# A cross-attention block on one core: steps over two pairs, seven products in more places, and the division moved from the weights to the context

## The chip, the cores and the metric

The kernel runs on one core of a Trainium2 chip. Its engines work side by side: TensorE (PE, with its weight loads as PEld), VectorE (DVE), ScalarE (ACT), GpSimd (POOL), and SyncE (SP), whose queue issues nearly all transfers. The metric is the device time of one launch in microseconds, lower is better; times are medians of runs.

## The reference

128 sequences of 128 tokens with 256 features attend to 128 sequences of context, with 16 heads of 16 features, and pass a feed-forward block with 1024 hidden features. All is float32.

```python
q = (query @ Wq + bq)    # heads: 16 x 16
k = (key @ Wk + bk)
v = (values @ Wv + bv)
scores = einsum('bhqd,bhkd->bhqk', q, k) / sqrt(16)
scores = where(j < i, scores, -1e30)          # mask == 0: strictly below the diagonal
attn = softmax(scores); attn[:, :, 0, :] = 0
ctx = einsum('bhqk,bhkd->bhqd', attn, v)
x = layer_norm(query + ctx @ Wo + bo, ln1_g, ln1_b)
ffn = relu(x @ W1 + b1) @ W2 + b2
out = layer_norm(x + ffn, ln2_g, ln2_b)
```

## The kernel before

Two sequences make a pair of 256 token columns; there are 64 pairs. Nothing loops on the chip: the program is written out in full, and the order in which each engine gets its instructions is the order in which Python emits them. The middle, pairs 7 to 62, is made of steps. One step (`steps`, from slot 9 to 60) runs the table `order` once: about 130 short names, each with a lag that says how many pairs back it works. The work on one pair is thus spread over several steps: scores and exponentials in its own step, the weighing of values at the end of the next, output and first norm two steps behind, H (W1) three behind, S (W2) four behind, the second norm five behind, and the store after that. The start and the end are written out call by call.

The names, with what they do for one pair:

- `q261`, `q457`, `q3`: the queries (class `Query`). The 256x256 matrix is cut into four 128x128 blocks and the 256 columns into two halves, and the product of the two by two blocks is made of seven block products instead of eight (1 to 7), with sums of blocks of Wq (once, `wqs`) and sums of the token blocks (`qs02`, `qs1`, `qs3`, on POOL, tile qS). DVE puts the seven together (`qC1`, `qU3`, `qC2`, `qC12`).
- `k`, `v`, `out`: keys, values and the output, four products of 256 columns each (`project`, `values`, `attention_out`). ACT copies the keys to kT four times (`copy_keys`, two halves of heads with zeros in between), the values to vz and vd.
- `H1` to `H7` (class `Hidden`): W1 by seven products; the two halves are the two sequences of the pair, so a matmul has 128 columns, and there are 4 x 7 of them. POOL makes the sums xS (`xs0` to `xs3`), ACT and DVE put the products together in hT, ACT adds the bias and takes the relu (`relu0` to `relu7`).
- `S1` to `S7` (class `Second`): W2 by seven products of four matmuls each, with sums hS on POOL (`hs0` to `hs3`). Six no-ops per pair are strewn between them on PE (`empty`).
- `scores`: 64 matmuls in strips of 32 rows, in all eight PSUM banks; `low`, `mask`, `max`, `lowmax` on DVE; `exp` and `lexp` on ACT with the row sums; `rcp` on DVE, and `sum0` to `sum2` on POOL, which multiply the weights (tile sm) by the reciprocals of their sums; `turn0` to `turn2`, transposes on DVE; `br0` to `br12`, sixteen transfers across partitions to pT; then `weigh` (tile pc) and `ctx`, ACT's copy of it to cxT.
- `tbx`, `x1out`, `x1in`: the normed tokens are transposed on DVE, written to DRAM by four transfers (x1t) and read back (x1T) for H.

The line that `Hidden` spends its matmuls on, and the one that POOL divides the weights by:

```python
ps[:, i * P : (i + 1) * P].rearrange("p (n a) -> p n a", a=32),
left(i), right, start=(i == 0 and which not in self.ONTO),
...
rs[:, :, None].to_broadcast([P, part.stop - part.start, n]), ALU.mult,
```

## Time and profile before

| | |
|---|---|
| median of 3 runs | 1477.11 us (1476.67 to 2419.54) |
| span of the profiled execution | 1476.5 us |
| granted TensorE clock in it | 0.999 |
| transfers | 206.22 MB, 140 GB/s in the mean |
| step of one pair in the middle | 22.45 us |

The profiled execution is the one whose spans and rows are quoted below. In the 40 slices of its span PE shows nine tenths or more in all but the last, POOL and DVE eight or nine in the middle, and ACT nine:

```profile
PE   9999999999999999999999999999999999999998
PEld 7788999999999999999999999999999999999998
DVE  7999899999998998998998999989989999999866
ACT  5758999999999999999999999999999999999863
POOL 7788999999999999999999999999999999999987
```

Rows of the chain give the start, the duration, the engine, the tile written, the line and the count of instructions. Rows of groups give line, engine, operation, tiles, shapes and count, then busy us and mean ns of one, then the idle time ahead of them and what ended it.

### The profile page before, as it was taken

What the parts mean: (1) busy time and instruction counts of PE and PEld (TensorE: products, weight loads), DVE (VectorE), ACT (ScalarE), POOL (GpSimd) and SP (SyncE); (2) the same over time, 40 slices, a digit from 0 to 9 for tenths busy, and PEclk for the clock granted to TensorE, in tenths of its full rate; (3) what the DMA queues carried; (4) which work ended last, traced back from release to release, by engine and by line L of the source; (5) the groups of instructions that cost most, each with busy time, mean ns of one, the idle gap of its engine ahead of it and who ended that gap; (6) DMA issues with size and microseconds to landing.
All of it is one profiled execution on the core that took longest, in us unless ns stands there. A gap on an engine that the chain in (4) does not pass through costs nothing.

```text
span 1476.5 us, 53972 instructions
## 1 busy us (share of the span) xinstructions
PE 1463.9 (99%) x19696; PEld 1377.8 (93%) x19696; DVE 1315.5 (89%) x2897; ACT 1323.0 (90%) x5279; POOL 1388.2 (94%) x1484
## 2 busy tenths in 40 slices
PE   9999999999999999999999999999999999999998
PEld 7788999999999999999999999999999999999998
DVE  7999899999998998998998999989989999999866
ACT  5758999999999999999999999999999999999863
POOL 7788999999999999999999999999999999999987
PEclk9999999999999999999999999999999999999999
DMA  8465566655656666666556566556565666664451
GB/s 203 96 141 127 133 146 139 147 138 136 156 141 138 141 146 139 148 144 145 138 135 154 139 142 141 144 135 157 141 139 136 146 141 150 136 152 122 116 162 58
DMA packets 417865, 206.22 MB, mean 140 GB/s; under 512 B 282434, under 2 KB 386114, under 8 KB 417602
## 3 DMA queue, kind: packets, MB, share of 16 engines
q1 hardware_dynamic: 416080, 202.49, 58.3%
q8 instruction: 159, 2.61, 0.8%
q14 instruction: 106, 0.85, 0.2%
q10 hardware_dynamic: 1520, 0.27, 0.1%
HBM read 71.84 MB, written 34.87 MB: 72 GB/s over the span
## 4 chain that ended last, share of the span: by engine, by line
PE 95%; DVE 1%; POOL 1%; DMA 1%; SPq 1%; issue 1%; ACT 0%; DVEq 0%; POOLq 0%
PE phs L1156 25%; PE pX L1064 11%; PE po L671 7%; PE pk L281 7%; PE pz L1064 7%; PE py L1064 7%; PE pv L411 7%; PE pq L351 6%; PE pss L502 6%; PE pc L652 4%; PE pc L642 3%; PE ph L917 1%; PE pq L281 1%; PE py L940 1%; SPq L608 1%; POOL sm L557 1%
## 5 line engine op out<-in xcount | busy, mean ns | idle before, releaser
L557 POOL TENSOR_TENSOR sm<-sm,rs 128x1024 f32<-128x1024 f32 x192 | 364.0, 1898 | 2.4 <-DVE rs L566 2.3
L997 ACT ACTIVATE sm<-pss,nmx 128x128 f32<-128x128 f32 x944 | 331.9, 395 | 8.4 <-DVE nmx L980 2.4
L997 ACT ACTIVATE sm<-sm,nmx 128x64 f32<-128x64 f32 x944 | 321.4, 361 | 0.8 <-DVE nmx L987 0.2
L1190 ACT ACTIVATE hT<-hT,b1e_c 128x256 f32<-128x256 f32 x480 | 216.1, 501 | 53.9 <-DVE hT L1181 44.7
L574 DVE STREAM_TRANSPOSE tb<-sm 128x1024 f32<-128x1024 f32 x186 | 227.8, 1226 | 1.5 <-POOL sm L557 1.4
L997 ACT ACTIVATION_READ_ACCUMULATOR sm<-pss,nmx 128x1 f32 x912 | 214.7, 235 | 0.0
L997 ACT ACTIVATION_READ_ACCUMULATOR sm<-sm,nmx 128x1 f32 x912 | 193.8, 212 | 0.0
L1156 PE MATMUL phs<-xS,w1t 128*128 128x128 f32 x1440 | 180.2, 275 | 0.0
L1156 PEld LDWEIGHTS phs<-xS,w1t 128*128 128x128 f32 x1440 | 170.4, 192 | 0.0
L980 DVE TENSOR_REDUCE nmx<-pss 128x4 f32<-128x512 f32 x236 | 160.6, 682 | 1.9
L401 ACT ACTIVATE kT<-pk,bkh,half 128x256 f32<-128x256 f32 x252 | 140.0, 559 | 4.1 <-PE pk L281 4.1
L516 DVE TENSOR_TENSOR sm<-pss,neg 128x256 f32<-128x256 f32 (+1 forms) x276 | 113.8, 436 | 16.5 <-PE pss L502 12.5
L1064 PE MATMUL pX<-wt,hS 128*128 128x128 f32 x960 | 126.8, 275 | 0.0
L1156 PE MATMUL phs<-x1T,w 128*128 128x128 f32 x960 | 126.5, 275 | 0.0
L1156 PEld LDWEIGHTS phs<-x1T,w 128*128 128x128 f32 x960 | 120.7, 192 | 3.0
L671 PE MATMUL po<-wo,cxT 128*128 128x256 f32 x512 | 121.8, 381 | 0.0
L411 PE MATMUL pv<-wv,cT 128*128 128x256 f32 x512 | 120.9, 379 | 0.0
L281 PE MATMUL pk<-cT,wk 128*128 128x256 f32 x504 | 119.5, 380 | 0.0
L1064 PEld LDWEIGHTS pX<-wt,hS 128*128 128x128 f32 x960 | 117.0, 192 | 0.1
L411 PEld LDWEIGHTS pv<-wv,cT 128*128 128x128 f32 x512 | 96.9, 190 | 13.1
L671 PEld LDWEIGHTS po<-wo,cxT 128*128 128x128 f32 x512 | 92.5, 190 | 12.2 <-issue 1.6
L281 PEld LDWEIGHTS pk<-cT,wk 128*128 128x128 f32 x504 | 91.5, 190 | 10.5 <-issue 0.2
(192 smaller groups left out, 4149.3 us busy)
## 6 DMA issues: line engine op xcount, KB each, us to landing
pT<-tb SPq DMA_DIRECT2D x976, 96.0 KB, 2.3
x1t<-tbx SPq DMA_DIRECT2D x252, 64.0 KB, 2.7
x1T<-x1t SPq DMA_DIRECT2D x63, 256.0 KB, 3.4
out_dram<-t SPq DMA_DIRECT2D x63, 256.0 KB, 4.3
xb<-in_x_dram SPq DMA_DIRECT2D x124, 128.0 KB, 3.3
cb<-in_ctx_dram SPq DMA_DIRECT2D x124, 128.0 KB, 3.2
x<-in_x_dram SPq DMA_DIRECT2D x31, 512.0 KB, 5.0
w<-in_L_xattn_W_dram SPq DMA_DIRECT2D x2, 1024.0 KB, 7.8
```

Source lines behind the costliest of these rows:

```text
L281: nc.tensor.matmul(ps[:, m * TP : (m + 1) * TP], w[:, k, m * P : (m + 1) * P], src[:, k, :], start=(k == 0), stop=(k == KC - 1),)
L401: nc.scalar.activation(st["kT"][:, m, e, :], pk[:, m * TP : (m + 1) * TP], AF.Identity, bias=bkh[:, m, e : e + 1], scale=half[:, e : e + 1],)
L411: nc.tensor.matmul(pv[:, s * D : (s + 1) * D], st["cT"][:, k, s * P : (s + 1) * P], wv[:, k, :], start=(k == 0), stop=(k == KC - 1),)
L516: nc.vector.tensor_tensor(probabilities(p, hi)[:, 4 * r : 4 * r + 4, :], st["sps", hi][r][:, : 4 * n].rearrange("p (n j) -> p n j", j=n), ...
L557: nc.gpsimd.tensor_tensor(sm[:, part, :], sm[:, part, :], rs[:, :, None].to_broadcast([P, part.stop - part.start, n]), ALU.mult,)
L574: nc.vector.transpose(st["tb"][:, :, at : at + 256].rearrange("p j (n a) -> p n j a", a=32), probabilities(p, hi).rearrange("p h j -> p (h ...
L671: nc.tensor.matmul(po[:, s * D : (s + 1) * D], cxT[:, k, s, :], wo[:, k, :], start=(k == 0), stop=(k == KC - 1),)
L980: nc.vector.tensor_reduce(maxima(p, 1)[:, 4 * r : 4 * r + 4], st["sps", 1][r].rearrange("p (n j) -> p n j", j=P), AX.X, ALU.max, negate=True,)
L997: nc.scalar.activation(sm[:, h, :], src, AF.Exp, bias=nmx[:, h : h + 1], scale=1.0, **({"accum_out": st["su", hi][:, h : h + 1]} if summed ...
L1064: nc.tensor.matmul(out, left(k), right(k), start=(first and k == 0), stop=(k == K - 1), skip_group_check=True,)
L1156: nc.tensor.matmul(ps[:, i * P : (i + 1) * P].rearrange("p (n a) -> p n a", a=32), left(i), right, start=(i == 0 and which not in self.ONT ...
L1190: nc.scalar.activation(self.hT[:, f], self.hT[:, f], AF.Relu, bias=b1e_c[:, f : f + 1], scale=1.0,)
```

## The change

One step now goes over two pairs (a group), 25 steps from `steps(5, 30)`, with a table of some 290 entries (name, which pair of the two, lag in steps). In it:

- H, queries and keys run by seven products over two pairs: one half of the columns is the first pair, the other the second, so a matmul has 256 columns. H is split in two halves of W1's columns (`a`, `b`), each in banks of its own.
- Values run by seven products over two pairs, with matmuls of 128 columns; the output by seven in a pair, likewise.
- Products 1, 6, 7 and 4 gather in one bank, which ACT or DVE reads between them (`keep`, or `add` for the output); 2, 5 and 3 are added by DVE.
- Keys are kept once; the second set with zeros is made from them, half on POOL, half on ACT (`kc0` to `kc3`).
- The weights are not divided. The reciprocals of the sums (`rcp`) are transposed on DVE (`rT`), written to DRAM (`rout`), read back as 8 rows of 512, each spread over 16 partitions (`rin`, tile R, 256 KB) and multiplied into the context by DVE (`divide`) in place of ACT's copy.
- qT, kT, hT, hS and the loads have one buffer for two pairs each. The loads of x, context and tokens for a group are emitted once per step.
- No no-ops are emitted with S.

```diff
-                bufs=n,
+                bufs=1,
...
+    CHAIN, TWO_BANKS = (1, 6, 7, 4), {2: 0, 5: 1, 3: 1}
...
+        def sides(self, w, raw, comb):
+            a = lambda m, k: block(self.w, m, k)
+            t = lambda n: combination(self.w, self.ws, n)
+            return {
+                1: lambda: (a(0, 0), raw(0, 0)), 2: lambda: (a(0, 1), raw(1, 0)),
+                3: lambda: (t(3), raw(1, 1)), 4: lambda: (a(1, 1), comb(3)),
+                5: lambda: (t(0), comb(0)), 6: lambda: (t(1), comb(1)), 7: lambda: (t(2), comb(2)),
+            }[w]()
...
+    class Square(Seven):
...
+            nc.tensor.matmul(
+                self.at(w), left, right, start=first, stop=True, skip_group_check=True,
+            )
+
+        def keep(self, n):
+            m, u = ((0, 0), (0, 1), (1, 1), (1, 0))[n]
+            nc.scalar.activation(
+                self.out[:, m, u], self.at(1), AF.Identity, bias=self.bias[:, m : m + 1], scale=1.0
+            )
+
+        def add(self, w):
+            m, u = {2: (0, 0), 5: (1, 1), 3: (0, 1)}[w]
+            nc.vector.tensor_tensor(self.out[:, m, u], self.out[:, m, u], self.at(w), ALU.add)
...
+    class Values(Seven):
...
+            for s in range(2):
+                nc.tensor.matmul(
+                    self.at(w)[:, s * P : (s + 1) * P], left[:, s * P : (s + 1) * P], right,
+                    start=first and s == 0, stop=True, skip_group_check=True,
+                )
...
+    class Output(Seven):
+
+        AT = {1: (0, 0), 6: (0, 0), 7: (0, 0), 2: (1, 0), 4: (1, 1), 5: (2, 0), 3: (2, 0)}
...
+    def spread_keys(g, m, e):
+        kT = states["joint", g]["kT"]
+        if m in KEYS_ON_POOL:
+            nc.gpsimd.tensor_tensor(
+                kT[:, m, e], kT[:, m, 1],
+                half[:, e : e + 1, None].to_broadcast([P, 2, TP]), ALU.mult,
+            )
...
+    def divide(p):
+        view = lambda t: t.rearrange("p (m l s i) -> p m l s i", m=KC, l=2, s=2)
+        pc, by = view(states[p].pop("pc")), view(states[p].pop("R"))
+        nc.vector.tensor_tensor(
+            cxT[:, :, :, 0, 1:], pc[:, :, 0, :, 1:], by[:, :, 0, :, 1:], ALU.mult
+        )
+        nc.vector.tensor_tensor(cxT[:, :, :, 1], pc[:, :, 1], by[:, :, 1], ALU.mult)
...
+    def leave_sums(p):
+        st = states[p]
+        mid = st["mid R"] = dram.tile([32, NS, 32], F32, tag="R", name=f"Rm_{p}")
+        nc.sync.dma_start(mid.rearrange("h b a -> b h a"), st.pop("rsT"))
+
+    def fetch_sums(p):
+        st = states[p]
+        st["R"] = keeping(proj, "R", [P, KC * TP])
+        mid = st.pop("mid R").rearrange("(x y) b a -> x (y b a)", x=8)
+        nc.sync.dma_start(st["R"], mid[:, None, :].to_broadcast([8, DK, KC * TP]))
...
+            for n in range(2):
+                nc.tensor.matmul(
+                    ps[:, n * TP : (n + 1) * TP].rearrange("p (s i a) -> p s i a", s=2, a=32),
+                    left(2 * r + n), right, start=(n == 0 and which not in self.ONTO),
+                    stop=True, skip_group_check=True,
+                )
...
+            nc.scalar.activation(
+                self.hT[:, f, 1], self.one(4, i // 2)[:, i % 2], AF.Relu,
+                bias=b1e_c[:, f : f + 1], scale=1.0,
+            )
...
+    PADS = 0
...
+        ("S6", 1, 2), ("kk1", 0, -1), ("ks2", 0, -1), ("shifts", 1, 1), ("tbx", 0, 1),
+        ("K7", 0, -1), ("qk1", 0, -1), ("bo", 0, 0), ("lexp4", 1, 0), ("turn1", 1, 0),
...
+    def steps(first, last):
+        for slot in range(first, last):
+            for name, half, lag in order:
+                run(name, slot - lag if name in of_two else 2 * (slot - lag) + half)
...
+    steps(5, 30)
```

How this moves instructions is shown at three places. The numbers in the names are pairs (or groups, for pk, pq, pv, pa, pb and pd) and buffers.

On PE, behind the scores, before: queries, output, queries, S, keys and values of one pair follow.

```order
L351 MATMUL pq_34_0_11533<-xT_34_11238,wq_85 128x128
L351 MATMUL pq_34_0_11533<-qS_34_11447,wqs_185 128x128
L671 MATMUL po_31_11547<-wo_110,cxT_182 128x256 x4
L351 MATMUL pq_34_1_11554<-qS_34_11447,wq_85 128x128
L351 MATMUL pq_34_1_11554<-qS_34_11447,wqs_185 128x128 x2
L1064 MATMUL pX_29_11560<-w2_137,hT_29_11252 128x128 x4
L281 MATMUL pk_34_11567<-cT_34_11344,wk_83 128x256 x4
L411 MATMUL pv_33_11611<-wv_93,cT_33_10981 128x256 x4
```

On PE, behind the scores of the first pair of a group, after (pa, pb and pd are the banks of H, po those of the output, nS the sums of the normed tokens, oS those of the context).

```order
L1382 MATMUL pb_14_1_10586<-x1T_28_10467,w1_126 128x256 x2
L1382 MATMUL pa_14_0_10595<-x1T_28_10467,w1_126 128x256 x2
L531 MATMUL po0_30_10599<-wo_110,cxT_165 128x128
L1382 MATMUL pa_14_1_10609<-x1T_28_10467,w1_126 128x256 x2
L1382 MATMUL pb_14_0_10623<-x1T_28_10467,w1_126 128x256 x2
L531 MATMUL po0_30_10599<-wos_171,oS_1775 128x128
L1382 MATMUL pa_14_0_10595<-nS_2478,w1t_173 128x256 x2
L1382 MATMUL pa_14_1_10609<-nS_2478,w1t_173 128x256 x2
L1382 MATMUL pd_14_1_10663<-nS_2478,w1t_173 128x256 x2
```

H of the group two steps back stands there now, with matmuls of 256 columns, its first two products from x1T, the sixth (the seventh row) from nS; single output products stand between.

On DVE, from the transpose of the normed tokens to the first masks, before:

```order
L882 STREAM_TRANSPOSE tbx_30_11383<-t1_30_11229 128x4x4x32
L1184 TENSOR_TENSOR hT_29_11252<-hT_29_11252,phs_29_5_11337 128x4x128
L574 STREAM_TRANSPOSE tb_32_11314<-sm_32_11164 128x8x4x32
L516 TENSOR_TENSOR sm_33_11529<-pss0_33_2_11491,neg_156 128x256
L516 TENSOR_TENSOR sm_33_11529<-pss0_33_3_11492,neg_156 128x256
L516 TENSOR_TENSOR sm_33_11529<-pss0_33_0_11489,neg_156 128x256
```

And after, the last rows ahead of the first masks of a group's first pair (the turn of the weights writes wide0 here, the division reads pc and R):

```order
L1322 TENSOR_TENSOR t2_29_10707<-t2_29_10707,pz_29_11022 128x2x128
L334 STREAM_TRANSPOSE xT_36_11136<-xb_36_10947 128x512
L454 TENSOR_TENSOR qT_219<-qT_219,pq1_17_10998 128x256
L767 STREAM_TRANSPOSE wide0_270<-wide1_509 128x8x4x32
L1322 TENSOR_TENSOR t2_29_10707<-t2_29_10707,py_29_11110 128x128
L864 TENSOR_TENSOR cxT_165<-pc_32_11160,R_1700 128x4x63
L867 TENSOR_TENSOR cxT_165<-pc_32_11160,R_1700 128x4x64
L709 TENSOR_TENSOR wide3_371<-pss0_34_2_11217,neg_139 128x256
```

The two rows of the division now stand directly ahead of the masks, and the transposes of the normed tokens (tbx, both pairs of the group) some 17 and 9 rows ahead of it.

On SP, the transfers of one step before (pT the weights across partitions, x1t and x1T the normed tokens out and in):

```order
L256 DMA x1t_40_15098<-tbx_40_15023 32x4x128 x4
L608 DMA pT_42_15103<-tb_42_14954 32x768 x4
L262 DMA x1T_40_15108<-x1t_40_15098 128x4x128
L608 DMA pT_42_15103<-tb_42_14954 32x768 x12
L93 DMA cb_46_15122<-in_ctx_1024_dram 32x32x32 x4
```

And after, about half of those of a step over two pairs:

```order
L801 DMA wide3_371<-wide2_476 32x768 x8
L1224 DMA Rm_32_11020<-rsT_32_10980 4x32x32
L801 DMA wide3_371<-wide2_476 32x768 x4
L323 DMA x1t_30_11093<-tbx_1006 32x4x128 x4
L801 DMA wide3_371<-wide2_476 32x768 x4
L1230 DMA R_1700<-Rm_32_11020 128x1x512
L323 DMA x1t_31_11139<-tbx_1006 32x4x128 x4
L329 DMA x1T_30_11144<-x1t_30_11093 128x4x128
L329 DMA x1T_31_11150<-x1t_31_11139 128x4x128
L801 DMA wide2_476<-wide0_270 32x768 x8
```

The reciprocals go out and come back among the weights' transfers, and x1out and x1in of the two pairs now stand together, with the next pair's weights behind them.

More of the change, by code (lines that the diff above doesn't have):

```diff
@@ L936, in second @@
         st = states[p]
-        if s == 0 and fs[0] == 0:
-            st["py"] = at_bank(6, f"py_{p}")
+        once("py", p, lambda: at_bank(HOMES.get(f"py_{p}", 6), f"py_{p}"))
         for f in fs:
@@ L1516, in tile_cross_attention_block, with hidden7, one_pair, two_pairs @@
-    ops, order = step_tables()
-    def steps(first, last):
-        for slot in range(first, last + 1):
-            for name, lag in order:
-                if 6 < slot - lag < NP - 1:
-                    ops[name](slot - lag)
+        return once("second", p, lambda: Second(p, PADS))
+    def hidden7(g):
+        return once("hidden", ("joint", g), lambda: Hidden(g))
+    ops, of_two = {}, set()
+    def one_pair(**more):
+        ops.update(more)
+    def two_pairs(**more):
+        ops.update(more)
+        of_two.update(more)
@@ new lines, in tile_cross_attention_block @@
+    mask(3, 1, (0,))
+    run("qk0", 2)
+    mask(3, 1, (2,))
+    attention_sum(1)
+    x1_blocks(0)
+    x1_untile(0, 0)
+    scores(3, 0)
+    mask(3, 0, (3,))
+    x1_untile(0, 1)
+    run("Q6", 2)
+    mask(3, 0, (2,))
+    mask(3, 0, (1,))
+    hidden(0, 2)
+    sums(2, 0, ALL)
+    spread_values(3, (0,))
+    stats(1, states[1]["t1"], 1)
+    hidden(0, 4)
+    deviation(1, 1)
+    turn(2, 1, 1)
+    hidden_relu(0, 3)
+    run("K1", 2)
+    run("qk1", 2)
+    maximum(3, 1, ONE)
+    run("loadc", 3)
@@ new lines, in tile_cross_attention_block @@
+    run("Q2", 2)
+    less(3, 1, ONE)
+    stack_values(3, (0,))
+    hidden_relu(0, 4)
+    turn(2, 0, 0)
+    turn(2, 1, 0)
+    hidden_relu(0, 5)
+    run("qs3", 2)
+    run("kk0", 2)
+    run("ks3", 2)
+    hidden(0, 0)
+    run("Q5", 2)
+    mask(3, 0, (0,))
+    maximum(3, 1, TWO)
+    hidden_relu(0, 0)
+    hidden_relu(0, 2)
+    less(3, 1, TWO)
+    spread_values(3, (1,))
+    maximum(3, 0, ALL)
+    run("K6", 2)
+    exponential(3, 1, ONE)
+    less(3, 0, ALL)
+    totals(3, 1, ONE)
+    run("kk1", 2)
@@ new lines, in tile_cross_attention_block @@
+    sums(3, 1, TWO)
+    run("kk2", 2)
+    bring(2, nc.sync, EVERY[8:12])
+    run("Q4", 2)
+    totals(3, 0, ALL)
+    run("qa5", 2)
+    run("qk3", 2)
+    sums(3, 0, ALL)
+    second(0, 1)
+    run("K4", 2)
+    leave_x1(1)
+    turn(3, 1, 0)
+    residual1(0, nc.gpsimd, (0,))
+    turn(3, 1, 1)
+    run("ka5", 2)
+    turn(3, 0, 0)
+    second(0, 0)
+    run("K3", 2)
+    combine_square("q", (3,))
+    weigh(2)
+    run("xT", 6)
+    run("Q3", 2)
+    context(2)
+    attention_out(2)
+    scale_w1((0,))
```

3781 lines of the change are left out of this document (2107 added, 1674 removed), and 119 rows, old and new, of tables (BANKS, HOMES, order).

## The prediction

> **What bounds the kernel now.** I read the page's busy times first, then the busy times of a single step in the middle, then the chain of work that ended last through one step, and last the groups and tiles that the change touches.
>
> ```profile
> PE 1463.9 (99%) x19696; PEld 1377.8 (93%) x19696; DVE 1315.5 (89%) x2897; ACT 1323.0 (90%) x5279; POOL 1388.2 (94%) x1484
> ```
>
> ```profile
> 722.89:745.34 22.45, 22.45 (x315) 21.42 (x318) 20.43 (x47) 21.25 (x89) 21.65 (x24) 1.00 0.66 154
> ```
>
> The second fence is one step of one pair from the middle: its start and end, its length, the busy time of PE, PEld, DVE, ACT and POOL, the granted clock, the DMA share and GB/s. PE has no gap: 22.45 of 22.45 us. The others stand idle 2.02 (DVE), 1.20 (ACT) and 0.80 us (POOL). So a microsecond of PE work is a microsecond of time, as long as the other three and the transfers keep up. The chain through that same step is PE alone, and prices every product:
>
> ```profile
> 722.89 0.36 PE pc L642 x16
> 723.25 0.45 PE pc L652 x32
> 723.70 0.22 PE pc L642 x16
> 723.92 0.45 PE pc L652 x32
> 724.37 1.52 PE pss L502 x45
> 725.90 0.86 PE pq L351 x6
> 726.76 1.73 PE po L671 x8
> ...
> 729.16 0.89 PE pX L1064 x8
> 730.05 1.73 PE pk L281 x8
> 731.78 1.73 PE pv L411 x8
> ...
> 740.87 4.47 PE phs L1156 x40
> ```
>
> Each written matmul is two instructions. A 128-column one costs 4.47/20 = 0.2235 us, a 256-column one 1.73/4 = 0.4325 (less than two narrow ones by 0.0145). The query products that follow the scores take 0.19 more than three narrow ones (0.86); that stays, whatever product comes first there. The S products carry the no-ops and cost 0.89 for four, as the H products without them do (4.47/5), so the no-ops cost nothing and their removal gives nothing.
>
> **The change on PE.** Per pair, in us, and times the pairs that get it:
> - H: 28 narrow (6.26) become 14 wide (28 wide for two pairs; 6.055): 0.203 x 60 pairs = 12.2
> - keys: four wide (1.73) become 3.5 wide (1.514): 0.216 x 60 = 13.0
> - values, and output: four wide become seven narrow (1.5645): 0.1655 x 60 = 9.9 each
> - queries: seven narrow become 3.5 wide: 0.051 x 55 = 2.8; five pairs more leave the four wide: 1.1
> - S: one pair more by sevens (16 wide to 28 narrow): 0.7
>
> Together 49.6 us; a step over two pairs has 2 x 21.65 = 43.3 us of PE work where two steps had 44.9. From the profiled execution's 1476.5 that leaves 1426.9; the runs' median is 0.6 above the span, so 1427.5 if nothing new waits. Only PE's page row says that start and end are bound by PE too (12.6 us of the whole span are not PE); I leave those 12.6 as they are.
>
> By the Trainium skill (TensorE: Matmul & The Clock Gate, section "Back-to-back issue gap") a warm matmul takes its columns plus a fixed 2.5 ns. The chain's two passes per matmul have a fixed part of 0.0145/2 = 7 ns. An estimate with the page's figure would shrink the H term to about 4 us and queries to 1, and raise values and output to 12 each, for a time near 1433 ahead of any new wait. The rows decide here.
>
> **The other engines, per pair.** These rows are the same step by tile, hT, qT, kT and rs in turn (their columns as above; qT and kT without POOL, rs with DVE and POOL alone), and groups of the page:
>
> ```profile
> 722.89:745.34 22.45, 3.17 (x24) 2.92 (x24) 3.39 (x5) 4.76 (x11) 5.10 (x4) 1.00 0.66 154
> ```
> ```profile
> 722.89:745.34 22.45, 1.59 (x64) 1.32 (x64) 1.42 (x4) 0.35 (x1) 1.00 0.66 154
> ```
> ```profile
> 722.89:745.34 22.45, 1.59 (x64) 1.32 (x64) 0.00 (x0) 2.23 (x4) 1.00 0.66 154
> ```
> ```profile
> 722.89:745.34 22.45, 0.60 (x3) 5.69 (x3) 1.00 0.66 154
> ```
> ```profile
> L729 DVE TENSOR_TENSOR t<-po,xb 128x512 f32<-128x512 f32 x64 | 43.4, 679 | 4.1 <-PE po L671 4.1
> L516 DVE TENSOR_TENSOR sm<-pss,neg 128x256 f32<-128x256 f32 x256 | 101.5, 418 | 15.4 <-PE pss L502 12.5 <-PE pss L476 1.0
> L1088 DVE TENSOR_TENSOR t<-t,pX 128x128 f32<-128x128 f32 x120 | 32.5, 271 | 7.2 <-POOL xS L1110 0.8 <-PE pX L1064 0.5
> L664 ACT COPY cxT<-pc 128x508 f32<-128x508 f32 x64 | 37.3, 582 | 5.6 <-PE pc L652 4.0
> L1166 ACT COPY hT<-phs 128x512 f32<-128x512 f32 x60 | 34.0, 567 | 8.4 <-PE phs L1156 8.3
> L294 ACT ACTIVATE qT<-pq,bqs_c 128x256 f32<-128x256 f32 x14 | 6.8, 483 | 2.5 <-PE pq L281 2.5
> L320 POOL TENSOR_TENSOR qS<-xT 128x256 f32<-128x256 f32 x55 | 40.2, 730 | 0.0
> L324 POOL TENSOR_TENSOR qS<-xT,qS 128x128 f32<-128x128 f32 x55 | 25.2, 459 | 4.2
> L1025 POOL TENSOR_TENSOR hS<-hT 128x512 f32<-128x512 f32 x60 | 76.4, 1274 | 9.4 <-ACT hT L1190 9.4
> ```
>
> POOL loses the three products of weights and reciprocals (5.69). It gains the differences of cxT (0.73 + 2 x 0.46 = 1.65) and of cT (four of 128x256 for two pairs, 1.46) and two key halves of 128x512 for two pairs (1.27). The sums for queries and for H come to 1.46 each, about 0.2 to 0.4 less than they are. Net -1.8: 19.8 us.
>
> DVE loses the reciprocals (0.60), the output sum (0.68), the query sums (1.42) and the hidden sums (3.39), 6.09 in all. It gains six output sums (4 x 0.27 + 2 x 0.42 = 1.92), two for the division (0.84), 4.5 of 128x256 for q, k and v (1.88) and three of 128x512 (2.03). The reciprocal of 32 columns and the turn of it are not in the trace; between nothing and the 0.60 of the three small ones, I take 0.4. Net +1.0 by durations, about +0.6 when short ones overlap as they do now: 21.0 to 21.4 of 21.65.
>
> ACT loses the copy of cxT (0.58), the query keep, four key copies and the hidden tile's 4.76, together 7.92. It gains three keeps (1.70), six relus of which two are twice as wide (0.40 each now, 4.76 less two keeps over nine; 4 x 0.40 + 2 x at most 0.80 = 3.2), four keeps for q and k (1.93) and one wide key copy (at most 1.1): 7.9. It stays at or under 21.25.
>
> So all three remain under PE, DVE and ACT by 0.3 to 0.6 us: that is their cover, thinner than now. Input loads have one buffer instead of two; the x load is written about half a step (20 us) behind the transposes that free the buffer and as far ahead of its reader, so I cost it at nothing.
>
> **Transfers.** This is where I expect the new wait.
>
> ```profile
> L608 SPq DMA_DIRECT2D pT<-tb x976: 507/591/2024, 55.7 to 1409.1; - x196
> ```
> ```profile
> L256 SPq DMA_DIRECT2D x1t<-tbx x252: 303/432/1977, 67.5 to 1446.7; - x126
> ...
> DMA to landing us min/median/max: 1.6/2.7/4.0
> ```
> ```profile
> L262 SPq DMA_DIRECT2D x1T<-x1t x63: 376/451/1306, 70.7 to 1448.6; - x63
> ...
>   PE phs L1156: 1.5, 1
> ...
> DMA to landing us min/median/max: 2.6/3.4/5.3
> ```
>
> In the new SP order, from the end of the first pair's tbx: four x1t (4 x 0.432 = 1.73), four pT (2.36, to 4.09), R (0.45), four x1t of the second pair (last issued at 5.84, landed at 8.55), then x1T of the second pair, landed at 11.95, then two sums on POOL (2 x 0.73): 13.4. H6, the sixth product of H, needs them. On PE, from the product beside which the table writes that tbx: six wide key and query products, four of S (16 narrow), the weighing (1.48): 7.64; then scores and its 0.19 (1.71), four half products of H (3.46) and two of output (0.45), to 13.3, less the 0.7 us that tbx itself lasts (a 128x512 DVE instruction, 0.68 in L729's row) if it starts with them: 12.6. The table writes it behind the start of an S product of 0.89 us; if it starts with that, PE is there at 13.5. So H6 waits between 0 and 0.8 us in a step over two pairs. R (256 KB, as x1T) is issued at 4.09 and lands near 7.5, and the division is due at the end of the weighing, between 6.95 and 7.85: late by at most 0.55, in the same place, behind which all masks queue on DVE, the exponentials on ACT and the freed banks that H needs on PE. The two overlap. I take 0.3 us, below the middle, because DVE is nearly full and comes to its rows early rather than with a gap; x 25 steps = 7.5 us. The second pair's weights and R have 1 to 2 us to spare by the same sum, because their 16 issues (9.5 us) follow the x1T.
>
> Forecast: 1427.5 + 7.5 = 1435.
>
> By the Trainium skill (DMA: Bandwidth & Descriptors, section "Why a DMA increments its semaphore by 16 and not by 1") a transfer uses the largest number of engines up to 16 that divides the slowest dimension on both sides. R's source has 8 there, so it would use 8 of 16, which speaks for a late R. No row here shows such a transfer.
>
> **Rivals.** Three rows of the waits of before (who waited for whom, us in total, times, longest) bear on them:
>
> ```profile
> ACT hT L1190 <- DVE hT L1181: 44.7, 55, 3.3
> DVE qT L386 <- PE pq L351: 44.2, 55, 1.5
> DVE t L1088 <- PE py L1064: 24.3, 58, 1.7
> ```
> - *Late transfers decide.* If x1t and x1T each land halfway from median to longest (0.65 and 0.95 us more), H6 waits 1.6 us per step, 39 us: 1466. For it: no spare time by medians, and both transfers stand in the densest part of SP's order. Against it: PE now waits for x1T once in the whole run (the row under x1T's above).
> - *ACT keeps its idle time.* 21.25 busy and the present 1.20 idle are 22.45 a pair; with 0.3 less work 22.15, 15 us gained in 50 pairs, and start and end bound the same way: about 1462. Against it: 0.8 us a step (44.7 over 55) of that idle time is a wait for one hidden sum, and the new code reads the hidden part of the fourth product straight from PSUM.
> - *Slower: DVE becomes the bound.* Place: the division ahead of the masks. If DVE keeps its 2.02 us idle, 21.0 to 21.4 + 2.02 is 23.0 to 23.4 a pair, 0.6 to 1.0 above 22.45, 30 to 50 us over 50 pairs: about 1515. It decides from 1.0 us idle per pair for slower at all. Against it: 1.2 us a step of the present idle ((44.2 + 24.3) over 55 or 58) are waits for PE, which a full PE makes and which cost nothing.
>
> **How the numbers follow.** About 2% is what a measurement of this kernel can tell from no change: 1447.6 and 1506.7 are the bounds. Forecast (waits of 0 to 0.8 us a step, 1427 to 1447): 0.63. Late transfers: 0.15, a third of it still under 1447.6. ACT: 0.11. DVE: 0.09. The rest, 0.02, is start and end going otherwise. Faster 0.63 + 0.05, say 0.68; same 0.23; slower 0.09. The range goes from 1424 (no wait, a slightly shorter start) to 1466, which takes in both middle rivals.
>
> **What would show it.** Right: PE busy near 1411 to 1416 us; 0.4325 for each wide H, key and query product; POOL's group of 364.0 us gone to a handful; a step over two pairs of 43.3 us plus what PE idles ahead of the sixth H product; PE or POOL's sums waiting for x1T, DVE's division for R. Wrong: a step of 44 us or more with PE waiting for ACT or DVE at the scores; wide products over 0.44; x1T landing in good time with nothing waiting (then 1427); or DVE busy above 21.6 a pair.

## The result, and the profile after

| | before | after |
|---|---|---|
| median of the runs, us | 1477.42 (4 runs) | 1573.09 (4 runs, 1567.17 to 1583.39) |
| ratio to before, 95% interval | | 1.0655 [1.0609, 1.0702] |
| span of the profiled execution, us | 1476.5 | 1565.4 |

The change made the kernel 6.6% slower; the forecast was 2.9% faster. The ratios here and below leave out two slow executions, one of before (2419.54 us) and one of k3_order3_masks (1614.06 us). The profiled execution is the fastest of the four; against the prediction's sum without waits (1426.9 of span) 138.5 us are missing in it. Rows of the page of the changed kernel:

```profile
PE 1485.6 (95%) x18310; PEld 1317.0 (84%) x18310; DVE 1346.7 (86%) x3178; ACT 1325.9 (85%) x5303; POOL 1278.0 (82%) x1505
...
q8 instruction: 147, 2.41, 0.7%
...
PE 73%; DVE 8%; DMA 6%; SPq 6%; issue 4%; POOL 3%; ACT 1%; DVEq 0%; POOLq 0%; ACTq 0%
...
L695 PE MATMUL pss<-kT,qT 32*64 32x256 f32 (+1 forms) x3840 | 125.0, 335 | 25.5 <-issue 18.1
```

PE was 99% busy before and carried nearly the whole chain; now the other engines, DMA and SP's queue carry a quarter of it, and the scores (L695) have idle time in front that the profile can only call issue. The page's busy time misleads here: where PE stops inside a row of short matmuls, much of the stop counts as busy. Starts of instructions are safer. The scores of pair 11 start at 247.41 (before: 230.50), those of pair 61 at 1423.89 (before: 1352.79), so the 25 steps over two pairs and what lies around them can be cut apart. The busy times of each engine in start, steps and end, of after and then of before:

```profile
0.00:247.41 247.41, 220.93 (x2689) 186.11 (x2689) 200.81 (x410) 182.44 (x681) 192.91 (x229) 0.98 0.60 132
247.41:1423.89 1176.48, 1136.99 (x14306) 1018.47 (x14301) 1051.34 (x2523) 1054.76 (x4305) 980.26 (x1151) 0.99 0.66 148
1423.89:1565.40 141.51, 127.67 (x1329) 112.41 (x1322) 94.54 (x245) 88.67 (x320) 104.85 (x127) 0.98 0.40 103
```
```profile
0.00:230.50 230.50, 226.70 (x2809) 197.87 (x2809) 203.01 (x386) 177.41 (x574) 197.97 (x206) 1.00 0.61 140
230.50:1352.79 1122.29, 1122.29 (x15507) 1070.67 (x15501) 1021.27 (x2301) 1062.38 (x4401) 1082.51 (x1151) 1.00 0.61 142
1352.79:1476.50 123.71, 114.89 (x1394) 109.30 (x1388) 91.18 (x212) 83.22 (x306) 107.71 (x129) 0.99 0.43 116
```

A step takes 1176.48 / 25 = 47.06 us; the sum gave 43.3 and two pairs before took 44.9. So 94 of the 138.5 us are lost in the steps, and the other 44.5 in start and end (388.9 us, where the sum left 344.4). PE's weight loads (PEld) show the places in the steps. A row of waits gives who waited, for whom, the total idle time, how often and the longest:

```profile
PEld pss L695 <- issue: 24.0, 19, 2.6
PEld pss L695 <- PE pss L695: 11.1, 22, 1.2
```

More than half of the loss stands at the bursts of context products and scores, twice in a step. Before, every burst's scores took 1.52 us from their first start to the next product's. Now those of the even pair take 1.67 to 4.21 and those of the odd pair 2.10 to 3.81 us, in the mean 5.21 a step for both together, where two pairs took 3.05. Two places from one step (timeline: start, duration, engine; in brackets the idle time ahead). At the even pair R is in time, and yet PE stops for 0.66 us with 13 scores left:

```profile
744.55 1.57 PE L695 MATMUL pss<-kT,qT 32*64 32x128 f32 x51
744.76 0.42 DVE L864 TENSOR_TENSOR cxT<-pc,R 128x252 f32<-128x252 f32 x1 [0.59 <-PE pc L846]
746.77 0.66 PE L695 MATMUL pss<-kT,qT 32*64 32x128 f32 x13 [0.66 <-issue]
```

At the odd pair R is late, the division (L864, L867) starts 0.9 us after the scores, and the scores that need the divided bank wait for it:

```profile
762.68 1.12 PE L695 MATMUL pss<-kT,qT 32*64 32x128 f32 x32
763.59 0.42 DVE L864 TENSOR_TENSOR cxT<-pc,R 128x252 f32<-128x252 f32 x1 [1.40 <-DMA R<-Rm]
763.93 0.41 DVE L867 TENSOR_TENSOR cxT<-pc,R 128x256 f32<-128x256 f32 x1
764.49 1.09 PE L695 MATMUL pss<-kT,qT 32*64 32x256 f32 x32 [0.69 <-DVE cxT L867]
```

SP's queue behind that second place. A row is a run of issues of one line:

```profile
743.42 2.65 SPq L329 DMA_DIRECT2D x1T<-x1t  x2
746.17 6.07 SPq L801 DMA_DIRECT2D wide<-wide  x8
752.34 0.52 SPq L1020 DMA_DIRECT2D out_dram<-t  x1
752.92 2.41 SPq L801 DMA_DIRECT2D wide<-wide  x4
755.75 0.60 SPq L1224 DMA_DIRECT2D Rm<-rsT  x1
756.40 2.47 SPq L801 DMA_DIRECT2D wide<-wide  x4
758.97 0.65 SPq L1230 DMA_DIRECT2D R<-Rm  x1
```

From 743 to 759.6 SP has no free time to speak of. It stands in front of the second x1T until x1t has landed, then issues 16 transfers of weights at 0.6 to 0.8 us in the mean of a row, and R goes out last, 4.6 us ahead of the division that it holds up.

A first theory of the issue stops (theory P): the instruction queue q8 moved 2.41 MB in 147 packets, 16.4 KB each. PE's program comes in such pieces, by the count below of some 256 instructions. A burst has 96 passes of context products and 64 of scores, each a weight load and a matmul, 320 instructions in 3.0 us, so that inside a burst a piece lasts under 3 us; among 128-column products (64 x 0.22 us) it lasts 14. A piece began to arrive shortly before this stop:

```profile
q8 instruction: 1, 0.02, 10.0%
```

That is its row in the DMA view of 744.0 to 744.6; PE resumed at 746.77. At each of four such stops looked at, the piece's packet was seen 2.3 to 2.9 us before PE went on. By the program's list a step has 286 matmuls of four instructions each, 1144, and with those for waits about 1172; 115 pieces in 25 steps are 4.6 a step, 255 instructions each. Before, two pairs had 125 / 25 = 5.0 pieces, 1280 instructions, the 12 no-ops among them, so that the pieces ended at the same places of every two pairs.

### The profile page after: what moved, and what is told of

Read it like the earlier page. It is cut to its first block, busy times and chain, and to the rows that moved or that the text cites. A ratio compares the mean times of both kernels' runs of the same rounds, so it can differ in the third digit from the quotient of the medians.

```text
span 1565.4 us, 51401 instructions
## 1 busy us (share of the span) xinstructions
PE 1485.6 (95%) x18310; PEld 1317.0 (84%) x18310; DVE 1346.7 (86%) x3178; ACT 1325.9 (85%) x5303; POOL 1278.0 (82%) x1505
## 3 DMA queue, kind: packets, MB, share of 16 engines
q8 instruction: 147, 2.41, 0.7%
## 4 chain that ended last, share of the span: by engine, by line
PE 73%; DVE 8%; DMA 6%; SPq 6%; issue 4%; POOL 3%; ACT 1%; DVEq 0%; POOLq 0%; ACTq 0%
PE pa L1382 11%; PE pX L1298 10%; PE pz L1298 6%; PE py L1298 6%; PE pss L695 6%; PE pv L483 5%; PE pd L1382 5%; PE po L531 5%; PE pq L442 5%; PE pk L442 4%; SPq L801 3%; PE pb L1382 3%; PE pc L846 2%; DMA R<-Rm 2%; PE pc L837 2%
## 5 line engine op out<-in xcount | busy, mean ns | idle before, releaser
L1206 ACT ACTIVATE wide<-pss,nmx 128x128 f32<-128x128 f32 x960 | 341.0, 374 | 64.4 <-PE pss L695 40.7
L1206 ACT ACTIVATE wide<-wide,nmx 128x64 f32<-128x64 f32 x960 | 326.3, 352 | 0.7
L767 DVE STREAM_TRANSPOSE wide<-wide 128x1024 f32<-128x1024 f32 x186 | 227.8, 1227 | 1.0 <-ACT wide L1206 0.8
L1206 ACT ACTIVATION_READ_ACCUMULATOR wide<-pss,nmx 128x1 f32 x960 | 204.1, 213 | 0.0
L1206 ACT ACTIVATION_READ_ACCUMULATOR wide<-wide,nmx 128x1 f32 x960 | 195.7, 204 | 0.0
L695 PE MATMUL pss<-kT,qT 32*64 32x256 f32 (+1 forms) x3840 | 125.0, 335 | 25.5 <-issue 18.1
L1395 ACT COPY hT<-pa 128x512 f32<-128x512 f32 x180 | 103.9, 599 | 34.2 <-PE pa L1382 33.9
L695 PEld LDWEIGHTS pss<-kT,qT 32*64 32x64 f32 x3840 | 84.2, 131 | 52.9 <-issue 29.6
L709 DVE TENSOR_TENSOR wide<-pss,neg 128x256 f32<-128x256 f32 (+1 forms) x272 | 112.4, 430 | 15.7 <-PE pss L695 12.5
L1254 POOL TENSOR_TENSOR hS<-hT 128x512 f32<-128x512 f32 x61 | 77.6, 1272 | 56.1 <-PE py L1298 52.0
L1175 DVE TENSOR_TENSOR pss<-pss,neg 128x256 f32<-128x256 f32 x240 | 101.4, 423 | 24.4 <-PE pss L695 24.3
L1256 POOL TENSOR_TENSOR hS<-hT 128x512 f32<-128x512 f32 x61 | 78.3, 1283 | 29.1 <-ACT hT L1408 29.0
L998 POOL TENSOR_TENSOR t<-t,g_r 128x512 f32<-128x512 f32 x61 | 77.9, 1277 | 19.6 <-ACT t L991 19.6
L559 POOL TENSOR_TENSOR kT<-kT,half 128x512 f32<-128x512 f32 x60 | 62.4, 1040 | 34.7 <-DVE kT L454 32.4
```

The costliest lines, as they stand in the source:

```text
L695: nc.tensor.matmul(st["sps", hi][r][s * HP : (s + 1) * HP, m * 2 * n : (m + 1) * 2 * n].rearrange("p (e j) -> p e j", e=2), st["qT"][strip ...
L709: nc.vector.tensor_tensor(probabilities(p, hi)[:, 4 * r : 4 * r + 4, :], st["sps", hi][r][:, : 4 * n].rearrange("p (n j) -> p n j", j=n), ...
L767: nc.vector.transpose(st["tb"][:, :, at : at + 256].rearrange("p j (n a) -> p n j a", a=32), probabilities(p, hi).rearrange("p h j -> p (h ...
L1175: nc.vector.tensor_tensor(ps[:, :, HP:], ps[:, :, HP:], neg[:, 1, None, :].to_broadcast([P, 4, HP]), ALU.add)
L1206: nc.scalar.activation(sm[:, h, :], src, AF.Exp, bias=nmx[:, h : h + 1], scale=1.0, accum_out=su[:, at : at + 1],)
L1395: nc.scalar.copy(self.part(*((0, 0), (1, 0), (1, 1))[n], r), self.one(1, r))
```

## The experiments

In e3, m1 and m2 R is a tile of ones, so the weights stay undivided; in f1 and k2 the context is multiplied by the second norm's weights instead of R. These five leave out the division's values and are there for their times alone. Where no-ops are given, their number (53 to 55 a pair) is chosen so that a step has its 1280 instructions.

| run | what | median, us | ratio to before [95%] |
|---|---|---|---|
| after | the change | 1573.1 | 1.0655 [1.0609, 1.0702] |
| e1_pads | 1280 instructions a step by no-ops | 1575.8 | 1.0673 [1.0651, 1.0696] |
| e2_pads_shifted | the same, ends of pieces in the bursts | 1612.5 | 1.0920 [1.0873, 1.0967] |
| h1_before_nopads | before, without its no-ops | 1496.1 | 1.0122 [1.0107, 1.0137] |
| m1_noR_nopads | after without R's transfers | 1565.4 | 1.0586 [1.0564, 1.0608] |
| e3_no_R | e1 without R's transfers | 1534.5 | 1.0391 [1.0375, 1.0407] |
| f1_R_unread | e1, R read but not waited for | 1561.3 | 1.0582 [1.0556, 1.0608] |
| k2_R_quarter | f1 with a quarter of R's bytes | 1555.0 | 1.0550 [1.0508, 1.0593] |
| f2_R_on_ACT | e1, R issued by ACT | 1769.8 | 1.1973 [1.1947, 1.1998] |
| f3_SP_order | e1, SP's order moved | 1676.9 | 1.1351 [1.1332, 1.1370] |
| f4_order_masks | f3, masks and scores reordered | 1683.2 | 1.1398 [1.1381, 1.1415] |
| g1_order2 | e1, SP's order moved, store left | 1598.8 | 1.0820 [1.0804, 1.0837] |
| g2_order2_masks | g1, masks and scores reordered | 1592.9 | 1.0775 [1.0757, 1.0793] |
| g3_order2_nopads | g1 without no-ops | 1613.4 | 1.0914 [1.0895, 1.0934] |
| k1_order3 | g1, second x1T where it was | 1601.4 | 1.0821 [1.0780, 1.0862] |
| k3_order3_masks | k1, masks and scores reordered | 1594.5 | 1.0776 [1.0746, 1.0806] |
| e4_mask_order | e1, masks reordered otherwise | 1573.2 | 1.0638 [1.0595, 1.0682] |
| m2_noR_masks | e3, masks and scores reordered | 1529.3 | 1.0345 [1.0320, 1.0371] |

### Program pieces: no-ops that hold them in place

```diff
-        return once("second", p, lambda: Second(p, PADS))
+        return once("second", p, lambda: Second(p, 54 if p >= 6 else 0))
```

> The changed kernel, with 54 no-ops per pair between the matmuls of S from pair 6 on (108 per step over two pairs). Theory P (program pages): PE's program is loaded in pieces of 16 KB, 256 instructions; a step of the changed kernel has about 1172 instructions, so that the place where a piece ends wanders from step to step, and where it falls into the context products and scores (320 short instructions in 3.0 us) PE stops until the next piece is there: the idle time put down to issue, some 26 us at the scores. With 108 no-ops a step has 1280 instructions, five pieces, as two pairs of the kernel before had; the ends then stay where they were at slot 5, about 87 of 160 passes into the second pair's burst and 66 into the first's, where they cost nothing. P expects 1535 to 1552 us (26 to 35 less) and issue idle before the scores under 5 us. Rival theory R (late sums): the stops at the scores follow from R's late landing and the division behind it; no-ops change nothing: 1565 to 1580. Rival N: a no-op costs PE time of its own (10 ns each would be 27 us): 1590 or more.

In e2 one line more, ahead of the steps:

```diff
+    empty(128)
     steps(5, 30)
```

> The same, with 128 no-ops more in one place ahead of slot 5, which shifts every piece's end by half a piece for the rest of the run, into the first half of both bursts (23 and 2 of 160 passes). Theory P: now a stop of 1 to 2.5 us at nearly every burst, 50 of them: 50 to 100 us more than the run without the shift, 1590 to 1650. Rivals R and N: the same time as without the shift, within 5 us.

> The kernel before without its six no-ops per pair, nothing else. The prediction took them to cost nothing and their removal to give nothing: 1474 to 1480. Theory P: with them two pairs have 1280 instructions, five pieces, and the ends of the pieces stay in two places of the step; without them 1268, so that the ends wander through the bursts of context products and scores once in about 21 steps: 10 to 50 us slower, with idle time of PE put down to issue.

(Its edit: `Second(p - 4, 6)` becomes `Second(p - 4, 0)`.) PE's idle time ahead of the scores' weight loads, in e1, e2 and the kernel before without no-ops:

```profile
PEld pss L695 <- issue: 6.1, 6, 1.7
```
```profile
PEld pss L695 <- issue: 57.2, 45, 2.4
```
```profile
PEld pss L502 <- issue: 15.9, 20, 1.8
```

The place of the pieces does what theory P says: with 1280 instructions a step the stops go from 24.0 us in the steps to 3.2 (6.1 in the whole run), shifted by half a piece there are 45 of them, and before loses 18.7 us by the absence of its no-ops alone. The shift cost 36.7 us, less than the 50 to 100 expected. And e1's time did not fall, against my expectation of 26 to 35 us. Its waits of PE show what took the stops' place:

```profile
PE pb L1382 <- DMA x1T<-x1t: 17.5, 15, 2.5
PE pss L695 <- DVE cxT L867: 9.0, 13, 1.2
```

As PE came on time, x1T and R were late for it. That the no-ops themselves cost nothing is seen at the matmuls among them: four of S still take 0.89 us.

### R's transfers, and the two causes together

```diff
-        nc.sync.dma_start(mid.rearrange("h b a -> b h a"), st.pop("rsT"))
+        st.pop("rsT")
...
-        nc.sync.dma_start(st["R"], mid[:, None, :].to_broadcast([8, DK, KC * TP]))
+        st["R"] = ones_R
```

> The kernel with 54 no-ops per pair, but R is a tile of ones that was filled at the start: the sums' two transfers per pair (written to DRAM, read back to 128 partitions) are left out, and the context is multiplied by one instead of by the inverse sums. Theory R: the division waited for R in 7 of 50 places for 8.0 us in the steady part, and PE behind it; with the two issues of SP (1.25 us a pair) gone too, it is 10 to 30 us faster than the run with no-ops alone. Theory P: less than 10 us.

> The changed kernel without no-ops and without R's two transfers (R is a tile of ones; the division's values are left out, its instructions stay). With the no-ops this gave 1534.5. Theory P (program pieces cost time of their own once the transfers don't cover it): idle time of PE put down to issue at about half of the 50 bursts, 15 to 35 us more: 1550 to 1570. Rival (the pieces cost something only together with late transfers): within 5 us of 1534.5.

| | with R's transfers | without |
|---|---|---|
| ends of pieces wander | 1573.1 | 1565.4 |
| ends of pieces in place | 1575.8 | 1534.5 |

Taken alone, either edit gives 8 us or nothing; together they give 39. Leaving out R gave more than the 10 to 30 us expected once the pieces were in place. I read the table so: where a piece stops PE, R and x1T have that much more time, and where PE is on time, they are late. In m1 the stops are back in full:

```profile
PEld pss L697 <- issue: 33.7, 23, 3.2
```

With both gone a step is 1150.14 / 25 = 46.0 us, and the bursts of e3 are alike: even pair's scores 1.68, odd pair's 2.13 us, nearly everywhere.

```profile
240.70:1390.84 1150.14, 1130.83 (x14307) 1012.24 (x14301) 1047.93 (x2523) 1056.28 (x4305) 981.23 (x1151) 1.00 0.61 139
```

### What of R is dear: the wait, the bytes or the issue

f1 reads R as before, but the division multiplies by a resident row; k2 is f1 with `st["R"][:, :P]` as destination.

```diff
-        pc, by = view(states[p].pop("pc")), view(states[p].pop("R"))
+        pc = view(states[p].pop("pc"))
+        states[p].pop("R")
+        by = g2_r.rearrange("p (m s i) -> p m s i", m=KC, s=2)[:, :, None].to_broadcast([P, KC, 2, 2, 64])
```

> The kernel with 54 no-ops per pair (1575.8 us); the sums are still written to DRAM and R is read back, but the division multiplies by a resident row (the second norm's weights) and nothing waits for R. Without R's two transfers the time was 1534.5. Theory W (the wait for R itself is the loss): nearly all of the 41 us come back here too, 1535 to 1545. Theory Q (SP's queue and the DMA engines: 1.25 us of issue a pair and 512 KB a step that push x1T back): the time stays close to 1575, 1560 to 1578, with PE waiting for x1T as before.

> As the run in which R was read back but waited for by nobody (1561.3), with a quarter of R's columns read (64 KB instead of 256 KB, the same two issues per pair); the division again multiplies by the second norm's weights. Without R's two transfers the time was 1534.5. Theory bytes (the DMA engines' load makes x1T and the weights late): 1536 to 1546. Theory issue (SP's 1.25 us per pair and its order): 1553 to 1563.

Of the 41 us between e1 and e3 the wait is 14.5 (1575.8 to 1561.3). Three quarters of the bytes are 6 more, which the intervals do not tell from none. The last 20.5, from 1555.0 to 1534.5, go with the two issues a pair (0.60 and 0.65 us on SP), SP's stand for the sums before the first of them (18.2 us in k2) and the quarter of R's bytes that k2 still read. The bytes do reach x1T: SP stands in front of the second x1T, until x1t has landed, for 2.4 us in e1 and 2.5 in f1 (medians), and for 1.5 in k2 as in e3. Yet that one microsecond a step came with no more than the 6 us. That the rest is mainly room in SP's queue, taken from x1T and the weights, is the likeliest reading, but no run parts the issues from that last quarter.

### Moving the transfers

```diff
-        nc.sync.dma_start(mid.rearrange("h b a -> b h a"), st.pop("rsT"))
+        nc.scalar.dma_start(mid.rearrange("h b a -> b h a"), st.pop("rsT"))
...
-        nc.sync.dma_start(st["R"], mid[:, None, :].to_broadcast([8, DK, KC * TP]))
+        nc.scalar.dma_start(st["R"], mid[:, None, :].to_broadcast([8, DK, KC * TP]))
```

> The kernel with 54 no-ops per pair; the sums' write and R's read are issued by ACT instead of SP, so that they pass SP's queue by, and their packets go through another ring than the weights. Theory Q with SP's queue as its cause: 1540 to 1555, as SP is free of 2.5 us a step and R no longer stands behind the weights and x1. Theory Q with the DMA engines as its cause (the bytes are the same): within 10 us of 1575.8. ACT's own cost: ACT has some 4.6 us of 47 idle in a step; if an issue holds it as long as SP (0.65 us), it gets late: 1580 or more.

A wide miss: 194 us slower than e1. SP's waits:

```profile
SPq L801 <- DMA R<-Rm: 129.8, 26, 6.5
SPq L801 <- DMA Rm<-rsT: 97.2, 44, 4.9
```

In the program each issue takes one of eight completion semaphores in turn, whichever engine issues it, and waits until the last user of its semaphore has landed. The second queue did not free SP; SP now waits for transfers that ACT issues late. This run tells nothing about the room in SP's queue.

The other runs move rows of the table, in this form:

```diff
+    order = list(order)
+    for name, ahead in (
+        (("rout", 1, 1), ("mask3", 0, 0)),
+        (("br2", 1, 1), ("max3", 0, 0)),
...
+    ):
+        order.remove(name)
+        order.insert(order.index(ahead), name)
```

> The kernel with 54 no-ops per pair; SP's order alone is changed, by moves in the table: for the odd pair the sums leave before br2 and R is read before br1, and the store, which stands between them and waits for POOL's last product of the norm, goes behind R; for the even pair the sums leave before br0, R is read before br3, and the first pair's x1T before the second pair's x1 is sent. All transfers are the same. Theory Q with the order as its cause: R's wait ends 3 us earlier and x1T of the first pair 2 us earlier: 1535 to 1555. If SP's total issue time or the DMA engines are the cause: within 10 us of 1575.8.

> The changed kernel with 55 no-ops per pair (a step has the 1280 instructions of the run with 54), and SP's order moved without the store: for the odd pair the sums leave before br2, and br0 is issued before SP waits for the second pair's x1T; for the even pair the sums leave before br0, and the first pair's x1T is asked for before the second pair's x1 is sent. In the run with the store moved back the scores had no wait left (1.67 and 2.10 us) but POOL stood 5 to 9 us a step on the store and PE on POOL. Theory Q with SP's order as the cause: without the store's move a step comes to about 46 us: 1535 to 1550. Rival (SP's issue time and the DMA engines as such): within 8 us of 1575.8.

> The changed kernel with 54 no-ops per pair and SP's order as in the last run, but the second pair's x1T is asked for where the change put it (in the last run it went behind br0, landed late, and PE stood 45 us on POOL's sums of it). Moved are: the sums ahead of br2 and br0, and the first pair's x1T ahead of the second pair's x1. Theory Q, order as the cause: PE's 17.5 us before x1T of the first pair and part of the wait for R go: 1550 to 1565. Rival (SP has no room: what is moved forward makes another transfer late): within 8 us of 1575.8, or slower.

f3 took the waits from most of the scores (1.67 and 2.10 us), and lost 101 us. POOL's first write of a new tile (L965) waits until the store of the tile's old content has landed, and the sums for S stand behind it; PE waits 50.0 us for those sums, and 23.7 us for the transfers of the weights. Then g1 and k1, which leave the store: they came out 23 and 26 us slower than e1, where 26 to 41 and 11 to 26 us less were expected, and PE waits for POOL's sums of x1T. The row of f3, and those of g1 and k1:

```profile
POOL t L965 <- DMA out_dram<-t: 150.9, 25, 9.5
```
```profile
PE pa L1382 <- POOL nS L1348: 45.5, 25, 3.7
...
POOL nS L1348 <- DMA x1T<-x1t: 86.1, 29, 4.9
```
```profile
PE pa L1382 <- POOL nS L1348: 27.6, 24, 2.2
```

In k1 the first pair's x1T goes out 0.4 us ahead of the second pair's four x1t. In the step looked at, SP could then ask for the second x1T only 3.6 us after the last x1t's issue (757.67 to 761.23), where in e1 it was 2.4 in the median. So there the 256 KB ahead of the small transfers delayed them by more than its issue. The sums are not the whole loss of k1: stops put down to issue are back at its scores, 21.3 us in 15 places against 6.1 in e1, though a step still has five pieces; why is open. Whatever was brought forward made something else late: of the orders tried none is better than the change's own, and no version here beats the kernel before.

> The same order of SP without the no-ops (about 1170 instructions a step). Theory P (program pieces): the idle time put down to issue is back at the scores, some 26 us: 15 to 30 us more than the run with them, if the transfers no longer hide it. Rival (only transfers count): within 6 us of the run with the no-ops.

Under g1's order the no-ops are worth 14.6 us (1598.8 to 1613.4), a little under what was expected.

### The bank that the division holds

```diff
-        for strips, hi, m in (
+        last = [(two, 1, 0), (two, 1, 1), (one, 0, 0), (one, 0, 1)]
+        if p % 2:
+            last = last[2:] + last[:2]
+        for strips, hi, m in [
-            (two, 1, 0), (two, 1, 1), (one, 0, 0), (one, 0, 1),
-        ):
+            (two, 0, 0), (one, 1, 0), (two, 0, 1), (one, 1, 1), *last,
+        ]:
...
+        (("low2", 1, 0), ("mask1", 1, 0)),
+        (("low0", 1, 0), ("mask1", 1, 0)),
```

> The kernel with 53 no-ops per pair; for the odd pair the last two groups of the scores are exchanged (the bank that the context products of the same pair held is written last), and the masks behind the division are taken in the order in which the banks are wanted by V1 and S1 (mask1, low0, low2, mask3). Theory B (banks): the context's bank is now free only after DVE's division, 1.05 us behind the start of the scores, and V1 and S1 wait for masks that stand behind the division: 0.58 us at the scores and 0.59 at V1 and S1 in each step. B expects 15 to 28 us less than the run with no-ops alone. Rival: ACT's exponentials, whose maxima come later in the new order, pass the wait on; no more than 5 us less.

> The kernel before it in this list (SP's order), with the last two groups of the odd pair's scores exchanged and the masks after them in the order low2, low0, mask1, mask3, since V1's bank is freed by low2 and S1's by low0 (the earlier run with mask1 and low0 ahead of low2 held V1 up). Theory B (banks): 0.58 us at the scores and 0.1 to 0.3 at S1 in each step, 10 to 20 us less than the run with SP's order alone. Rival: ACT's exponentials get their maxima later and the wait is passed on; no more than 5 us less.

> The same order of SP, and for the odd pair the last two groups of the scores exchanged and the masks after them as low2, low0, mask1, mask3. Theory B (the context's bank is held until DVE has divided): 0.58 us at the scores and 0.1 to 0.3 at S1 in each of 25 steps, 10 to 20 us less than the run with SP's order alone. Rival: ACT's exponentials get their maxima later; no more than 5 us less, or slower.

> The first kernel of this list, with the last two groups of the odd pair's scores exchanged and the masks after them as low2, low0, mask1, mask3. Before, the same edit on another order of SP gave 6 us. Theory B: 5 to 20 us less than the first kernel of this list. Rival: within 4 us of it.

> The kernel with no-ops and without R's transfers (1534.5), with the last two groups of the odd pair's scores exchanged and the masks after them as low2, low0, mask1, mask3. With R out of the way theory B shows its whole price: scores of the odd pair at 1.7 instead of 2.12 us and S1's 0.33 gone: 1515 to 1525. Rival: V1 waits for low2, which still stands behind the division's 0.83 us; what the scores gain, V1 loses: within 5 us of 1534.5.

V1 and S1 are the first products of the values and of S. e4's order put low2, which frees V1's bank, third, and held V1 up: no gain (1573.2 against 1575.8, where the intervals overlap). The later order gave 6.0 (g2), 6.6 by the ratios (k3, where the intervals overlap) and 5.1 us (m2), and cost 6.3 on f3 (f4). In m2 V1's 0.49 us went, but the odd pair's scores still took 2.13. The starts of single matmuls show why. Before, the second half of the 256-column scores starts 0.70 us into the burst; in e3 it starts 1.11 us into it, 0.15 us after the division's second row has ended, in 23 of the 25 odd pairs. In this burst of e3 the first half's loads are done at 746.88 and the second half's wait until 747.30:

```profile
746.22 0.66 PEld L697 LDWEIGHTS pss<-kT,qT 32*64 32x64 f32 x32
746.77 0.41 DVE L869 TENSOR_TENSOR cxT<-pc,ones_R 128x256 f32<-128x256 f32 x1
747.30 0.67 PEld L697 LDWEIGHTS pss<-kT,qT 32*64 32x64 f32 x32 [0.41 <-PE pss L697]
```

The program keeps the odd pairs' context in bank 2, which is one of that half's banks. In m2 the same matmuls start at the same 1.11 us, again 0.15 us after the division, in 22 of 25. The exchange brought only the narrow scores forward (from 1.17 to 0.94 us); the wide ones, which end the burst, still wait for the same row. So theory B is right on what holds the scores, and its cure could not reach them: the bank would have to be another one, or the division earlier. No run tried either.

## Why the prediction was wrong

1. *Prices of matmuls*: right. By the starts of rows a wide matmul takes 0.43, a narrow one 0.22 us, and the fixed part of some 7 ns a pass held. Wrong is what was made of them: a sum of prices was taken for the time of a step. In e3, with the pieces in place and without R's transfers, PE still loses 2.7 us a step (46.0 against 43.3) in small waits. Counted over its 25 steps from each product's start to the next one's, and against the prices of before, they are 0.94 at the scores (0.6 of it at the odd pair's in nearly every step), 0.49 at the values, 0.45 each at S and H, 0.29 at the weighing, 0.28 at the queries and 0.17 at the output: 3.07, of which the sum already held 0.38. 25 x 2.7 = 68 us are the largest part of the miss. Another 26 us in the steps are what pieces and R's transfers cost the changed kernel together (1176.48 against 1150.14), and the other 44.5 stand in start and end. The prediction carried over "The query products that follow the scores take 0.19 more ... that stays, whatever product comes first there". That step failed. Behind the odd pair's scores V1 in the place of the queries waits for a mask on DVE (L1175), which now stands behind the division, and the scores themselves wait for the division's bank. One burst of the changed kernel with R in time:

```profile
716.60 2.18 PE L695 MATMUL pss<-kT,qT 32*64 32x128 f32 x64
716.79 0.42 DVE L864 TENSOR_TENSOR cxT<-pc,R 128x252 f32<-128x252 f32 x1 [0.68 <-PE pc L846]
717.13 0.41 DVE L867 TENSOR_TENSOR cxT<-pc,R 128x256 f32<-128x256 f32 x1
717.69 0.42 DVE L709 TENSOR_TENSOR wide<-pss,neg 128x256 f32<-128x256 f32 x1
718.03 0.42 DVE L1175 TENSOR_TENSOR pss<-pss,neg 128x256 f32<-128x256 f32 x1
718.71 0.52 PEld L483 LDWEIGHTS pv<-wv,cT 128*128 128x128 f32 x4 [0.39 <-DVE pss L1175]
```

2. *"The no-ops cost nothing and their removal gives nothing"*: the first half is right, the second failed. They kept the pieces of PE's program in place: 18.7 us in the kernel before (h1), 31 us in the changed one without R (1534.5 to 1565.4).
3. *Other engines*: right. In the steps DVE is busy 1051.34 / 50 = 21.0 us a pair (21.0 to 21.4 predicted), ACT 21.1 (at most 21.25), POOL 19.6 (19.8). So neither DVE nor ACT became the bound, as two of the rivals had it. DVE did lose the time at the place that the slower rival named, the division ahead of the masks, but by its place in the order and not by its load; that rival's 1515 was nearer than the forecast.
4. *Transfers*: half of the place was right, the size was not. DVE's division did wait for R. But the sum had the sixth H product wait for POOL's sums of the second pair's x1T, and those waits of PE are 1.2 us in all of e1; PE waited 17.5 us there at the first H product (pb), for the first pair's x1T, which the sum did not follow. 0.3 us a step were taken. With the pieces in place, R's transfers cost 1.07 us a step: steps of 1176.94 us in all with them (e1) and of 1150.14 without (e3), 26.8 of the 33.4 us between these two spans. "The second pair's weights and R have 1 to 2 us to spare" failed: R of the odd pair was the late one. The sum let SP wait for x1t, but put the 16 weights at 9.5 us; in the step shown above their rows take 11.0, and with the store, the sums' write and a stop of 0.4 us before it R went out 12.9 us behind the second x1T. Where the division waited for R in the changed kernel (11 times), it began 4.0 to 5.4 us after R's issue, in this step 4.6 (758.97 to 763.59), where 3.4 was taken for the landing. Whether its source's 8 rows cause that, as the prediction took from the Trainium skill (DMA: Bandwidth & Descriptors, section "Why a DMA increments its semaphore by 16 and not by 1"), was not tried; the weights issued ahead of it are as good a reason.
5. *Start and end*, given 0.02 and a gain of some 10 us: 34.7 us longer than before instead (388.9 against 354.2), of which PE's plain idle time grew by 28 (12.6 to 40.3). Two stops in the start are 11.6 of it:

```profile
PE pq L348 <- DVE xT L334: 7.8, 1, 7.8
PE pk L442 <- DVE kT L454: 3.8, 1, 3.8
```

   In the first, PE stands until 31.61 for transposed tokens; DVE had stood 8.4 us for a load of context ahead of them. The longest of before's waits in its start is 1.5 us. What brought these loads late, and whether a step over two pairs fills and drains in coarser pieces, no run tested; it stays open.

So the slower side, which got 0.09, was under-rated. I take it that PE had 99% because its order, its pieces and SP's queue were fitted to each other, and all three were changed at once; for the pieces alone h1 shows it.

## What to carry to other kernels

When an engine is at 99% and its order is rewritten, price the handovers and not only the instructions: for each place where it comes to a bank or a tile, name the reader that must finish first and what now stands ahead of that reader. Instructions that do nothing may hold the program's pieces in place, so count instructions per loop step before taking them out. When several late things meet at one place, remove them together as well as one by one: here the removals alone read as 8 us and as nothing, and both together as 39 us.

## What the runs showed of the hardware

- PE's program comes in pieces of 16.4 KB, and a burst of short matmuls can outrun them: stops of up to 3.2 us at a burst (m1), 57.2 us in all of e2. The Trainium skill (Runtime: NRT & Kernel Launch, section "Instruction fetch mechanics") says the same of the blocks, 16 KiB and 256 instructions, and that crossing one is mostly hidden. The traces agree on the size of the blocks. In before, with the ends held in place, no crossing shows (every burst's scores in its steps take 1.52 us); in these bursts it is not hidden.
- A stop of PE can cost a second time. After 1.95 us without PE the granted clock (the third column from the right) was 0.50 for 6.8 us, from 1045.39 to 1052.21; the step with it took 49.3 us. The stretches around it in the changed kernel:

```profile
1042.70:1044.65 1.95, 0.00 (x1) 0.00 (x1) 0.00 (x0) 1.95 (x6) 0.26 (x1) 1.00 0.66 94
1044.65:1046.88 2.23, 2.23 (x59) 1.80 (x66) 1.46 (x4) 0.42 (x3) 0.94 (x2) 0.67 0.73 168
1046.88:1052.88 6.00, 6.00 (x47) 5.23 (x34) 4.39 (x15) 1.82 (x9) 4.79 (x6) 0.56 0.83 173
```

  Two more such stretches of 3.4 us, at 0.50, follow stops in the steps; behind the longest stop in the steps (2.37 us, to 606.38) the clock stayed at 1.00. The Trainium skill (TensorE: Matmul & The Clock Gate, section "Part 1: The HAM clock gate") knows the full and the half rate alone; the 0.50 agrees. The mean clock of this run is 0.991, by an estimate (0.009 x 1565.4) worth some 14 us, against 0.999 or 1.0 in before; in f2 it fell to 0.945.
- No-ops on PE are free at 54 a pair strewn between 28 narrow matmuls: four of S with theirs still take 0.89 us in e3.
